# A compare tree over 36 chunks, and paired word steps, as single VectorE instructions

## The chip, the cores and the metric

The kernel runs on one core of one Trainium2 chip. The metric is the device time of one execution in microseconds. The core has five engines with queues of their own: TensorE (PE, matmuls and their weight loads), VectorE (DVE), ScalarE (ACT), GpSimd (POOL) and SyncE (SP), and DMA queues started by some of them. Each engine runs its queue in order; a semaphore makes an instruction wait for another engine's.

## What is computed

Four graph layers run one after the other on 16 graphs of 1024 nodes with 64 channels. Each begins with a layer norm and a ReLU and ends with a residual. The change lies in the first layer's aggregation, which takes for each node and channel three quantiles of the neighbours' values:

```python
vals = jnp.where(nd[..., None], x[:, None, :, :], jnp.inf)   # nd: thinned adjacency
s = jnp.sort(vals, axis=2)
nv = nd.sum(2)
for tau, w in zip((0.25, 0.5, 0.75), (0.25, 0.5, 0.25)):
    pos = tau * (nv - 1)
    lo, hi = floor(pos), ceil(pos)
    agg = agg + w * (s[lo] + (pos - lo) * (s[hi] - s[lo]))
out = x + agg                        # then a two-layer MLP, masked
```

The other three are a gated message layer, a message layer with tanh, and an attention layer. All read the adjacency, of which some 6% is ones.

## The kernel before

The graphs are taken in eight pairs. For a pair, sort_begin and sort_pair sort each channel's 1024 node values on VectorE (one channel of one graph per partition): a bitonic sort of 55 steps, three instructions a step (L771 to L775), and then the same steps backwards on rank codes (L803 to L813). neighbours thins the adjacency and builds the 0/1 matrix ndT on all engines; it also writes a transposed copy of the adjacency (a_d, L886 and L887). weights turns rank codes into fp8 words wt (L974).

select then works on one graph at a time, eight tiles of 128 nodes, two tiles (TG) to a group, so four groups a graph. For each tile, words does this:

- 48 matmuls of ndT with wt (L1096): the bits of a word say which of 11 ranks are present, and the sum counts neighbours below. ScalarE evicts them into y (L1104), 128 values in each of 36 chunks (CHUNKS): 16 for each of two quantiles (full, NQ = 16), and 4 more (rest) that are joined with the first 16 at the end. Further matmuls make nat (L1124) and pz (L1132).
- 36 transposes of y (L1149), from which ScalarE makes two signs (L1151) for every eight chunks.

lasts runs on VectorE: it writes y plus 2048 beside y (L1162) and takes a tree of maxima over each chunk (L1167), down to one word in z per node, channel and one of four statistics. places turns z into four masks with some 26 instructions on 512 words (L1019, L1021, L1024): counts of the word's bits, three steps of a search for the place of the wanted rank. values multiplies the signs with tables (L1196; 40 matmuls for one statistic, 32 for the next) into candidates in PSUM, of which there are two buffers (pool sc), and VectorE picks from 12 candidates to one by copies under the masks (L1204) and adds it to agg (L1071, L1073). PSUM tiles named comb, of which there are four, hold the word sums, the transposes and the rest.

After the last words of a graph, compact gathers up to 64 exceptional nodes (L1235 to L1298, with 56 matmuls at L1287), and after both graphs extras treats them with their own maxima (L1007) and one call of places; its input comb_x is loaded on ScalarE's DMA queue (L1307), which also carries the stores of a_d. Then the four layers run for both graphs (L1459 and others read the adjacency as adjT), while neighbours, sort_pair and sort_begin of the next pairs run beside them.

The order on each engine is not written out by hand. The program states the work in order, with a priority, and a scheduler places every instruction on its engine's queue when its own model finds the operands ready; so the sort of the next pair stands in VectorE's queue between the instructions of select. The lines that set the order of the work around the change are these:

```python
now = words(0)
z = lasts(now[0])
for g in range(NT // TG - 1):
    values(g, now[1], places(sw, z, nf))
    now = words(g + 1)
    if g + 2 < NT // TG:
        z = lasts(now[0])
compact(b, i, wt, row10, out_of, kept, sw, sp)
values(g + 1, now[1], places(sw, lasts(now[0]), nf))
```

Of the kernel before, what the change touches and what calls it, by code (L numbers as in the profile page):

```python
# [13 lines left out]
U16 = mybir.dt.uint16  # L14
I16 = mybir.dt.int16
# [3 lines left out]
ALU = mybir.AluOpType  # L19
# [4 lines left out]
P = 128  # L24
# [18 lines left out]
def gnn_stack(ctx, tc, x, adj, nodemask, w, out):  # L43
# [952 lines left out]
    SHR, SHL, AND, XOR = ALU.logical_shift_right, ALU.logical_shift_left, ALU.bitwise_and, ALU.bitwise_xor  # L996
# [15 lines left out]
    def places(sw, z, nf, kept=2):  # L1012

        def word(name, bufs=1):
            return sw.tile([P, nf], U16, name=name, bufs=bufs)

        def bits(dst, src, v0, o0, v1=None, o1=None):
            if v1 is None:
                nc.vector.tensor_single_scalar(dst, src, v0, op=o0)  # L1019
            else:  # L1020
                nc.vector.tensor_scalar(dst, src, v0, v1, op0=o0, op1=o1)  # L1021

        def both(dst, p, q, op):
            nc.vector.tensor_tensor(dst, p, q, op=op)  # L1024

        zf = z.rearrange("p t s c -> p (t s c)")
        m, r, a, s0, s1, u1, u2 = (word(f"w_{n}") for n in ("m", "r", "a", "s0", "s1", "u1", "u2"))
        f1, f2, f, e0 = (word(f"w_{n}", kept) for n in ("f1", "f2", "f", "e0"))
        bits(m, zf, 1, SHL, 0xFFE, AND)
        bits(r, zf, 11, SHR, 31, XOR)  # L1030
        bits(s0, m, 1, SHR, 0x555, AND)
        both(a, m, s0, ALU.subtract)
        bits(s0, a, 2, SHR, 0x333, AND)
        bits(s1, a, 0x333, AND)
        both(s1, s0, s1, ALU.add)
        bits(s0, s1, 8, SHR)
        bits(s1, s1, 4, SHR, 15, AND)
        both(s1, s1, s0, ALU.add)
        both(u1.bitcast(I16), r, s0, ALU.subtract)
        both(u2.bitcast(I16), r, s1, ALU.subtract)  # L1040
        both(r, r, u1, ALU.min)
        both(r, r, u2, ALU.min)
        bits(f1, u1, 13, SHR, 4, AND)
        bits(f2, u2, 13, SHR, 4, AND)
        both(s0, f1, f2, ALU.add)
        both(m, m, s0, SHR)
        both(a, a, s0, SHR)
        bits(s1, a, 2, SHR, 3, AND)
        both(u1.bitcast(I16), r, s1, ALU.subtract)
        both(r, r, u1, ALU.min)  # L1050
        bits(f, u1, 14, SHR, 2, AND)
        both(m, m, f, SHR)
        bits(s0, m, 1, SHR, 1, AND)
        both(e0, s0, r, ALU.is_gt)
        return [v.rearrange("p (t s c) -> p t s c", t=z.shape[1], s=z.shape[2]) for v in (f2, f1, f, e0)]
# [25 lines left out]
    def select(b, i, wt, positive, ndT, row10, qb, qz, agg, kept, sw, sg, sy, sc, sp):  # L1081
        coef = row10[:, :, 3:9].rearrange("p t (k s) -> p t k s", s=2)
        if True:
# [74 lines left out]
            def lasts(ys):  # L1158

                z = sw.tile([P, TG, 4, C], U16, name="z", bufs=2)  # L1160
                for tl, y in enumerate(ys):
                    nc.vector.tensor_scalar_add(y[:, 1], y[:, 0], 2048.0)  # L1162

                    yu = y.bitcast(U16)
                    full, rest = yu[:, :, : 2 * NQ], yu[:, :, 2 * NQ :]
                    for v, n in ((full, 64), (full, 32), (full, 16), (full, 8), (rest, 64), (rest, 32), (rest, 16)):
                        nc.vector.tensor_tensor(v[:, :, :, :n], v[:, :, :, :n], v[:, :, :, n : 2 * n], op=ALU.max)  # L1167
                    zs = z[:, tl].rearrange("p (s k) c -> p s k c", k=2)
                    nc.vector.tensor_tensor(
                        zs[:, :, 1, :].rearrange("p s (q d) -> p s q d", d=4), full[:, :, NQ:, :4], full[:, :, NQ:, 4:8],  # L1170
                        op=ALU.max,
                    )
                    nc.vector.tensor_tensor(full[:, :, :NQ, :4], full[:, :, :NQ, :4], full[:, :, :NQ, 4:8], op=ALU.max)
                    for s in range(2):
                        nc.vector.tensor_tensor(
                            zs[:, s, 0, :].rearrange("p (m q d) -> p m q d", m=4, d=4),
                            full[:, s, :NQ, :4].rearrange("p (m q) d -> p m q d", m=4),
                            rest[:, s, :, :16].rearrange("p m (q d) -> p m q d", d=4), op=ALU.max,
                        )
                return z  # L1180
# [31 lines left out]
            nf = TG * 4 * C  # L1212
# [11 lines that stand above are left out]
# [77 lines left out]
    def extras(pr, kept, aggs, xs, xp):  # L1301
# [21 lines left out]
        for k in range(3):  # L1323
# [21 lines left out]
            nc.vector.tensor_tensor(zs, ev, od, op=ALU.max)  # L1345
            nc.vector.tensor_tensor(os_, od, ev, op=ALU.is_gt)
        marks = places(xs, z, 6 * C, 1)
        aggx = xs.tile([P, C], F32, name="agg_x")
        ag = aggx.rearrange("p (q d) -> p q d", d=4)
# [269 lines left out]
    for pr in range(pairs):  # L1619
        with tc.tile_pool(reuse_waits="tile", name="keep", bufs=1) as keep:  # L1620
            aggs = [keep.tile([P, NT, C], F32, name=f"agg{i}") for i in range(2)]
            kept = {
                "flag": [keep.tile([P, NT], U16, name=f"flag{i}") for i in range(2)],
                "vx": keep.tile([P, 9], F32, name="vx"),
            }
# [76 lines left out]
```

## Time and profile before

| | us |
|---|---|
| median of 3 runs (5891.88 to 5895.87) | 5891.98 |
| the profiled execution | 5867.21 |
| its span, first to last instruction | 5865.4 |
| VectorE busy (86%) | 5066.1 |
| TensorE busy (75%), its weight loads beside it | 4372.7 |
| ScalarE busy (65%) | 3801.4 |
| the tree, L1167, 896 instructions | 668.7 |
| the picks, L1204, 1536 instructions | 533.7 |
| granted TensorE clock, mean share of full speed | 0.84 |

Busy time is from one profiled execution. An instruction's duration runs from its start to its last write; the next one on the engine can start before that, so sums of durations come out above the time they fill. Lines such as L1167 are lines of the kernel before.

### The profile page before, as it was taken

The page shows a single profiled execution, that of the slowest core. Times are in us where ns is not written, and L with a number is a line of the kernel's source. Part 1 is how long each engine was busy: PE and PEld are TensorE (multiplying, and loading weights), DVE is VectorE, ACT ScalarE, POOL GpSimd, SP SyncE. Part 2 cuts the span into 40 slices and gives each one's busy share as a digit, 9 for nine tenths or more (in the row PEclk, how much of TensorE's full clock was granted, in tenths as well). Part 3 has the DMA queues.
Part 4 walks back from the last instruction along what each step waited for, and adds up shares of the span by engine and source line. Part 5 has one row for each costly group of instructions (what it writes and reads, how often), then busy time and mean ns, then how long its engine had stood idle before and what let it go on. Part 6 is the DMA issues. An engine that isn't in the chain of part 4 may idle for free.

```text
span 5865.4 us, 114417 instructions
## 1 busy us (share of the span) xinstructions
PE 4372.7 (75%) x45010; PEld 2736.6 (47%) x45010; DVE 5066.1 (86%) x13175; ACT 3801.4 (65%) x5752; POOL 180.9 (3%) x292
## 2 busy tenths in 40 slices
PE   1488677885868857788577876788677895878856
PEld 1355443554435544455434554355443554435532
DVE  9899888988899897998889988899888998877744
ACT  1587657676576855777567666677657775577724
POOL 3000000000000000000000000000000000000000
PEclk5699778997889968899689986899878997789967
DMA  4401273013631056210561125501264013620023
GB/s 127 125 27 41 89 221 116 27 31 124 207 98 36 20 156 217 63 40 29 172 203 45 37 77 168 172 35 34 89 206 132 27 32 120 208 81 19 11 88 127
DMA packets 524420, 568.23 MB, mean 97 GB/s; under 512 B 263808, under 2 KB 413568, under 8 KB 523872
## 3 DMA queue, kind: packets, MB, share of 16 engines
q1 hardware_dynamic: 381472, 476.43, 26.0%
q10 hardware_dynamic: 140064, 81.84, 4.6%
q8 instruction: 355, 5.82, 0.4%
q0 software_dynamic: 2336, 2.57, 0.2%
q14 instruction: 193, 1.58, 0.1%
HBM read 376.95 MB, written 183.76 MB: 96 GB/s over the span
## 4 chain that ended last, share of the span: by engine, by line
PE 27%; DVE 23%; ACT 14%; DMA 10%; issue 3%; SPq 0%; POOL 0%; ACTq 0%; DVEq 0%; POOLq 0%
PE comb L1096 7%; DVE y L1167 5%; PE cand L1196 4%; DMA adjT<-a_d 4%; PE bank L1459 4%; ACT sign L1151 3%; PE comb L1287 3%; DMA a_d<-at 2%; ACT y L1104 2%; DVE cand L1204 2%; DVE att L1570 2%; DVE adjT L1563 1%; DVE y L1162 1%; DVE cum L878 1%; DVE wt L974 1%
## 5 line engine op out<-in xcount | busy, mean ns | idle before, releaser
L1096 PE MATMUL comb<-wt,ndT 128*128 128x512 fp8e5 x6144 | 1422.3, 383 | 119.5 <-ACT sign L1151 98.1
L1104 ACT ACTIVATE y<-comb,qb 128x512 int16<-128x512 f32 x1152 | 742.5, 711 | 479.4 <-PE comb L1096 479.0
L1096 PEld LDWEIGHTS <-ndT 128*128 128x128 fp8e5 x6144 | 587.6, 98 | 837.4 <-issue 196.9
L1196 PE MATMUL cand<-vtab,sign 128*128 128x48 f16 (+1 forms) x18432 | 678.8, 192 | 60.9 <-DVE agg L1071 32.4
L1196 PEld LDWEIGHTS <-sign 128*128 128x128 fp8e5 x18432 | 651.5, 97 | 118.6 <-issue 57.2
L1151 ACT ACTIVATE sign<-comb,lower 128x1024 fp8e5<-128x1024 int16 (+1 forms) x640 | 693.2, 1083 | 0.0
L1151 ACT ACTIVATE sign<-comb,half 128x1024 fp8e5<-128x1024 int16 (+1 forms) x640 | 688.0, 1075 | 0.0
L1167 DVE TENSOR_TENSOR y<-y 128x512 uint16<-128x512 uint16 (+5 forms) x896 | 668.7, 788 | 16.6 <-PE comb L1149 16.2
L1204 DVE COPY_PREDICATED cand<-w_f,cand 128x256 f32<-128x256 uint16 (+1 forms) x1536 | 533.7, 376 | 95.8 <-PE cand L1196 92.6
L886 ACT COPY at<-pk 128x512 f32<-128x512 f32 x256 | 147.4, 586 | 394.5 <-PE pk L884 219.0
L1149 PE MATMUL comb<-ident_b,y 128*128 128x128 bf16 x4608 | 318.1, 222 | 93.5 <-ACT sign L1151 59.6
L1459 PE MATMUL bank<-adjT,nd 128*64 128x512 f32 x1024 | 314.1, 668 | 77.6 <-DMA adjT<-a_d 75.7
L1149 PEld LDWEIGHTS <-y 128*128 128x128 bf16 x4608 | 294.6, 99 | 118.9 <-issue 117.9
L928 PE MATMUL pk<-minus_b,rem 128*128 128x128 bf16 x1024 | 225.3, 246 | 158.2 <-ACT rem L909 158.2
L1459 PE MATMUL bank<-att,hs 128*64 128x512 f32 x512 | 199.9, 863 | 155.0 <-ACT hs L1575 154.9
L928 PE MATMUL pk<-ident_b,ni 128*128 128x128 bf16 x1024 | 220.5, 243 | 122.0 <-ACT ndT L934 65.0
L878 DVE TENSOR_TENSOR_SCAN cum<-ni 128x1024 f16<-128x1024 fp8e5 x128 | 291.8, 2283 | 11.0 <-POOL ni L874 10.9
L884 PE MATMUL pk<-ident,a 128*128 128x128 f32 x1024 | 189.5, 336 | 136.8 <-DMA a<-in_adj_dram 102.5
L974 DVE TENSOR_SCALAR wt<-node 128x2048 uint8<-128x2048 f16 x224 | 268.8, 1216 | 13.9 <-PE comb L1287 13.7
L774 DVE TENSOR_TENSOR s<-s 128x512 f32<-128x512 f32 (+1 forms) x440 | 275.6, 626 | 0.0
L1162 DVE TENSOR_SCALAR y<-y 128x4608 int16<-128x4608 int16 x128 | 173.4, 1355 | 118.0 <-ACT y L1104 117.7
L775 DVE TENSOR_TENSOR s<-s 128x512 f32<-128x512 f32 (+1 forms) x440 | 274.4, 624 | 0.0
(373 smaller groups left out, 8301.5 us busy)
## 6 DMA issues: line engine op xcount, KB each, us to landing
adjT<-a_d SPq DMA_DIRECT2D x384, 512.0 KB
a<-in_adj_dram SPq DMA_DIRECT2D x128, 512.0 KB
a_d<-at ACTq DMA_DIRECT2D x256, 256.0 KB
m_d<-swapped SPq DMA_DIRECT2D x104, 512.0 KB
swapped<-m_d SPq DMA_DIRECT2D x104, 512.0 KB
n_d<-nat SPq DMA_DIRECT2D x128, 128.0 KB
x_d<-xr SPq DMA_DIRECT2D x48, 256.0 KB
comb_x<-x_d ACTq DMA_DIRECT2D x24, 512.0 KB
```

Of the source, the lines that this page charges most:

```text
L774: nc.vector.tensor_tensor(to_lo, lo, hi, op=ALU.max)
L878: nc.vector.tensor_tensor_scan(cum[:, t - t0, :], ni[:, t, :], wide[:, t, pad - 1 : pad - 1 + N], 0.0, op0=ALU.add, op1=ALU.add)
L928: nc.tensor.matmul(pk[:, n % 4, :], lhs, rhs, start=(n % 4 == 0 and m == 0), stop=(m == len(terms) - 1 and last),)
L974: nc.vector.tensor_scalar(wt[g][:, :, k : k + 4, :].bitcast(U8), node, 4.0 * (25 + CODE * (8 * g + k)), 4.0 * 26, op0=ALU.add, op1=ALU.min,)
L1096: nc.tensor.matmul(pw, ndT[:, j, t * P : (t + 1) * P], wt[1 + g8][:, j].rearrange("p w c -> p (w c)"), start=(j == 0), stop=(j == NT - 1),)
L1104: nc.scalar.activation(y[:, 0, chunks, at : at + 8 * d_].rearrange("p q (w d) -> p q w d", d=d_), pw.rearrange("p (w q d) -> p q w d", w=8 ...
L1149: nc.tensor.transpose(pt[:, q - q0, :], y[:, 0, q, :].bitcast(BF16), ident_b)
L1151: nc.scalar.activation(signs[tl][s][:, q0:q1, :], pt.bitcast(I16), AF.Sign, bias=before[s], scale=-1.0, saturate=False,)
L1167: nc.vector.tensor_tensor(v[:, :, :, :n], v[:, :, :, :n], v[:, :, :, n : 2 * n], op=ALU.max)
L1196: nc.tensor.matmul(cand[:, e, at : at + 12 * d_].rearrange("p (d l) -> p d l", l=12), signs[tl][sec][:, chunk, :], tab[:, q, :, half_ * 12 ...
L1204: nc.vector.copy_predicated(v[:, :, :, dst : dst + k], mk.to_broadcast([P, 2, C // 2, k]), v[:, :, :, frm : frm + k])
L1459: nc.tensor.matmul(po[to : to + C, :], lhs, rhs[:, f * HALF : (f + 1) * HALF], start=(j == 0), stop=(j == NT - 1))
```

## The change

Three edits, all on VectorE:

- The tree's steps at 64, 32 and 16 run over all 36 chunks at once, where they ran over the 32 chunks of full and the 4 of rest in turn. The step at 8 stays as it is, since the chunks of rest end at 16 values.
- In places, m and a, s0 and s1, u1 and u2, f1 and f2 become the halves of four tiles of twice the width, and the two subtractions, the two sign extractions and the two shifts are one instruction each. The operand that both share, r or s0, is repeated with stride 0.
- Nothing else: the number of buffers stays (two for ff, f and e0; two PSUM tiles for the candidates), and so does the stated order of the work. The scheduler orders the queues anew for the changed list of instructions.

```diff
+        def two(name, bufs=1):
+            return sw.tile([P, 2, nf], U16, name=name, bufs=bufs)
+
+        def twice_(v):
+            return v.rearrange("p (o n) -> p o n", o=1).to_broadcast([P, 2, nf])
+
         zf = z.rearrange("p t s c -> p (t s c)")
-        m, r, a, s0, s1, u1, u2 = (word(f"w_{n}") for n in ("m", "r", "a", "s0", "s1", "u1", "u2"))
-        f1, f2, f, e0 = (word(f"w_{n}", kept) for n in ("f1", "f2", "f", "e0"))
+        r = word("w_r")
+        ma, ss, uu, ff = two("w_ma"), two("w_s"), two("w_u"), two("w_ff", kept)
+        m, a, s0, s1, u1, u2, f1, f2 = (v[:, k, :] for v in (ma, ss, uu, ff) for k in range(2))
+        f, e0 = (word(f"w_{n}", kept) for n in ("f", "e0"))
...
-        both(u1.bitcast(I16), r, s0, ALU.subtract)
-        both(u2.bitcast(I16), r, s1, ALU.subtract)
+        both(uu.bitcast(I16), twice_(r), ss, ALU.subtract)
         both(r, r, u1, ALU.min)
         both(r, r, u2, ALU.min)
-        bits(f1, u1, 13, SHR, 4, AND)
-        bits(f2, u2, 13, SHR, 4, AND)
+        bits(ff, uu, 13, SHR, 4, AND)
         both(s0, f1, f2, ALU.add)
-        both(m, m, s0, SHR)
-        both(a, a, s0, SHR)
+        both(ma, ma, twice_(s0), SHR)
...
                     full, rest = yu[:, :, : 2 * NQ], yu[:, :, 2 * NQ :]
-                    for v, n in ((full, 64), (full, 32), (full, 16), (full, 8), (rest, 64), (rest, 32), (rest, 16)):
+                    for v, n in ((yu, 64), (yu, 32), (yu, 16), (full, 8)):
                         nc.vector.tensor_tensor(v[:, :, :, :n], v[:, :, :, :n], v[:, :, :, n : 2 * n], op=ALU.max)
```

## The prediction

> **What bounds the kernel now.** I read the engine totals, then two stretches of the windows table, then the groups by shape, then the timeline of single engines, and last the order of the changed program's queues, which can be listed without running it. The profiled execution took 5867.2 us around a span of 5865.4; the median of the three timed runs is 5892.0, 0.4% above. I work in the profiled times and carry the difference over to the median.
>
> The totals (busy us, share of the span, instructions):
>
> ```profile
> PE 4372.7 (75%) x45010; PEld 2736.6 (47%) x45010; DVE 5066.1 (86%) x13175; ACT 3801.4 (65%) x5752; POOL 180.9 (3%) x292
> ```
>
> VectorE (DVE) is busiest, but an average hides that two kinds of group alternate in the selection stage. Two such groups, from the first L1162 of one to that of the next:
>
> ```profile
> core 0: us, PE busy (x) PEld busy (x) DVE busy (x) ACT busy (x) POOL busy (x), PEclk, DMA share, GB/s
> 378.60:419.70 41.10, 36.78 (x488) 24.21 (x488) 40.89 (x109) 33.17 (x55) 0.00 (x0) 1.00 0.06 21
> 5285.10:5324.00 38.90, 36.74 (x489) 24.27 (x489) 31.76 (x91) 33.40 (x55) 0.00 (x0) 1.00 0.03 8
> ```
>
> In the first ("dense") group the next pair's sort fills VectorE to 40.89 of 41.10 us: VectorE sets the period. In the second ("trailing") the sort has run out: VectorE idles 7 us, TensorE (PE) 2.2, and TensorE with its waits sets 38.9 us. The old queues hold 19 trailing groups (one in pair 0, two in each of pairs 1 to 6, six in pair 7); the other groups of pairs 0 to 6 are dense or hold a compaction.
>
> **What a merged instruction saves.** Mean ns per instruction stand after the bar; the run of seven is one whole old tree:
>
> ```profile
> L1167 DVE TENSOR_TENSOR y<-y 128x4096 uint16<-128x4096 uint16 x128 | 292.7, 2286 | 16.6 <-PE comb L1149 16.2
> ...
> L813 DVE TENSOR_TENSOR code<-code,xo 128x1024 uint16<-128x1024 uint16 x232 | 159.3, 686 | 4.1
> ...
> L1167 DVE TENSOR_TENSOR y<-y 128x512 uint16<-128x512 uint16 x256 | 105.1, 416 | 0.0
> ```
>
> ```profile
> 401.30 5.03 DVE L1167 TENSOR_TENSOR y<-y 128x4096 uint16<-128x4096 uint16 x7
> ```
>
> From 4096 and 512 elements: (2286 - 416) / 3584 = 0.522 ns an element, and 149 ns fixed. But the seven means of a tree add up to 5.52 us and the run lasts 5.03, so six successors each start 81 ns before the end of the one ahead. The issue slot's fixed part is 149 - 81 = 68 ns, and that, not 149, is what a merge saves. The change removes three instructions per tile in the tree (three pairs of seven become three of four; 128 tiles) and three per call of places (64 calls in selection, 8 in extras): 384 + 216 = 600, times 68 ns = 40.8 us of VectorE time. The elements stay. The operand repeated by stride 0 keeps its rate if it behaves as L813, which repeats one too and takes 686 ns for 1024 elements (0.522 x 1024 + 149 = 684).
>
> The Trainium skill (Perfetto Trace Analysis, Optimizing Scalar/DVE Operations) puts this overhead at about 60 ns, which would make 36 us, and advises grouping where the engine is saturated. The same section speaks against the change elsewhere: where VectorE is not saturated but holds up others, breaking instructions up may finish sooner; that is the trailing group.
>
> **What it adds: dependence.** The old tree alternated the 32 and the 4 chunks, so that no step followed the one it read. The new one is a bare chain. What such a pair costs is seen in the last extras, where nothing else was left to put between:
>
> ```profile
> 5619.85 0.25 DVE L1021 TENSOR_SCALAR w_r<-z_x 128x384 uint16<-128x384 uint16 x1
> 5620.02 0.25 DVE L1021 TENSOR_SCALAR w_s<-w_m 128x384 uint16<-128x384 uint16 x1
> 5620.30 0.36 DVE L1024 TENSOR_TENSOR w_a<-w_m,w_s 128x384 uint16<-128x384 uint16 x1
> ```
>
> w_s reads nothing of w_r and starts 0.17 us after it; w_a reads w_s and starts 0.28 us after it, though w_s took as long as w_r. A bare dependent pair loses 0.11 us. In the dense groups the new order puts a sort step or a pick between, so nothing is lost, but VectorE's order changes. In trailing groups nothing is left: a tree gains 3 x 0.068 and loses 3 x 0.11, so it ends some 0.1 us later. The Trainium skill (VectorE: DVE Perf Modes, The DRAIN you can't avoid) says a semaphore between vector operations costs nothing; by it the tree would end 0.2 us earlier, and the measured pair decides.
>
> **Dense groups.** VectorE loses 2 x 3 x 0.068 + 3 x 0.068 = 0.61 us a group, with as many sort instructions ahead of the second compaction as before (140 against 141 in the pair I counted). But the new queues also put V (L1196) later: after the 36 transposes (L1149) TensorE mostly runs 37 to 43 word matmuls (L1096) before the first 72 of V, where it ran 11 to 17, and VectorE takes the next L1162 in the middle of places. The next bound is TensorE: 36.78 busy, the waits on ScalarE that stay (0.28, 1.26 and 1.62 below) and some 0.6 at the second tile's transposes make 40.3; L1162 waits for the last eviction, and I take 40.6. That is 41.1 - 40.6 = 0.5 a group; bounds 0 and 0.61 x 2. Three groups ahead of the first compaction in seven pairs: -10.5 us. The group of that compaction and the one after it hold 0.61 each, and VectorE has idle time in the first; I take 1.0 a pair, -7 (bounds 0 and -14).
>
> **Trailing groups.** TensorE, first around the transposes of a dense group, then of a trailing one:
>
> ```profile
> 416.55 2.01 PE L1149 MATMUL comb<-ident_b,y 128*128 128x128 bf16 x32 [0.28 <-ACT y L1104]
> 419.82 0.38 PE L1149 MATMUL comb<-ident_b,y 128*128 128x128 bf16 x4 [1.26 <-ACT sign L1151]
> 421.83 3.90 PE L1096 MATMUL comb<-wt,ndT 128*128 128x512 fp8e5 x16 [1.62 <-ACT sign L1151]
> ```
>
> ```profile
> 5302.40 2.02 PE L1149 MATMUL comb<-ident_b,y 128*128 128x128 bf16 x32 [0.28 <-ACT y L1104]
> 5304.52 1.63 PE L1196 MATMUL cand<-vtab,sign 128*128 128x48 f16 x40
> 5305.98 0.39 PE L1149 MATMUL comb<-ident_b,y 128*128 128x128 bf16 x4
> 5306.99 0.96 PE L1196 MATMUL cand<-vtab,sign 128*128 128x48 f16 x32 [0.62 <-DVE agg L1073]
> 5307.80 2.92 PE L1096 MATMUL comb<-wt,ndT 128*128 128x512 fp8e5 x12
> ```
>
> The old trailing order hides the two sign waits behind V (40, then 32). The new order reads 36 transposes, V 40, 5 word matmuls, V 32, 12 word matmuls, in all its 24 groups of that kind (pairs 2 to 6 now have three). The last four transposes then wait for the first pair of signs, as in the dense group: about 5305.7. V's 40 end at 5307.2, the 5 words wait for the second pair (5307.7) and end at 5308.8. V's 32 need a candidate buffer. L1162 now stands ahead of the last steps of places and waits for the eviction until 5302.4; with its slot of 1.27, eight steps left of places and picks (1.7), the tree's first step (2.5) and one add (0.2) the second buffer comes free near 5308.1. So V starts at 5308.8 and ends at 5309.6, the 12 words at 5312.3. By the old order the same work (17 words) would be done at 5307.8 + 17 x 0.222 = 5311.6. The price is 0.7 us; bounds 0 and 2.3 (1.26 + 1.62 - 0.62). Nineteen groups: +13.3. Five groups change from dense (about 40.1) to this kind (39.6): -2.5.
>
> **Extras.** ScalarE's queue in pair 1:
>
> ```profile
> 1387.58 0.58 ACT L886 COPY at<-pk 128x512 f32<-128x512 f32 x1 [0.89 <-PE pk L884]
> 1389.11 0.58 ACT L886 COPY at<-pk 128x512 f32<-128x512 f32 x1 [0.95 <-DMA a_d<-at]
> 1389.14 0.96 ACTq L887 DMA_DIRECT2D a_d<-at  x2
> 1390.13 2.69 ACTq L1307 DMA_DIRECT2D comb_x<-x_d  x4
> ```
>
> The load of comb_x is issued behind eight copies and eight a_d stores; in the new order behind seven copies and six stores, the other two following it. It can go at about 1388.2, 2 us sooner, and ScalarE idles 10.9 us for it. Behind it wait the extras, then the layers, but the neighbours' work on ScalarE and the loads of a and adjT share that path; I take half, -1 in seven pairs, -7 (bounds 0 and -14). Extras' own places: 8 x 0.2 less some stalls, -1.
>
> **The sum.** -10.5 - 7 + 13.3 - 2.5 - 7 - 1 = -14.7 us: 5852.5 profiled, 5877 on the median.
>
> **Rivals.** (a) VectorE is the path everywhere that counts: all 40.8 us come off, 5851. For it, 86% busy; against it, the 7 us idle in trailing groups and over 45 in each pair's layers. (b) Slower: V behind the transposes exposes both sign waits in full, 24 x 2.3 = +55, with -28 of gains left, +27, 5919. It decides above (28 + 12) / 24 = 1.7 us a group; against it, the walk above, by which the second wait is mostly covered. (c) The change does not do what it says: an instruction with a repeated operand falls to one element a cycle. The subtraction and the shift, 2 x 1024 x 0.52 ns x 64 = +68 us, 5960. L813 speaks against it. (d) All is absorbed, 5892: gains end in L1162's wait for ScalarE.
>
> **How the numbers follow.** About 0.2% (12 us) is what a measurement of this kernel can tell from no change. Forecast 0.48, own range 5860 to 5892: 0.33 of it faster by over 0.2%, 0.15 within. (a) 0.13, faster. (d) 0.12, same. (b) 0.23 and (c) 0.04, slower. So faster 0.46, same 0.27, slower 0.27. The range for 8 in 10 reaches to (a) with a little more from comb_x below, 5846, and most of (b) above, 5912.
>
> **What would show it.** Right: 68 ns per merge (tree instructions of 4608, 2304 and 1152 elements near 2553, 1351 and 750 ns); dense groups near 40.6 us with VectorE waiting for L1104 at the shift; trailing ones near 39.6 with 1.3 us of sign wait ahead of the last four transposes; comb_x issued 2 us sooner. Wrong: dense groups at 41 or more, trailing ones at 38.9 or above 40.5, places instructions of 1024 elements near 1.2 us, or layers stretches that differ by more than 3 us a pair.

## The result and the profile after

The changed kernel takes 5984.7 us (median of 6 runs, 5980.5 to 5992.4) against 5889.3 us for the kernel before in the same session: 1.0164 times as long, 95% interval 1.0151 to 1.0177. The forecast was 5877, the range 5846 to 5912. The change is slower by 95 us, and the profiled span grew by 114.1 us, from 5865.4 to 5979.5. Lines behind L1058 stand five higher in the changed kernel (L1167 became L1172, L1096 L1101, L1149 L1154, L1196 L1201).

The totals after the change (busy us, share, instructions):

```profile
PE 4464.2 (75%) x45010; PEld 2767.7 (46%) x45010; DVE 5052.1 (84%) x12575; ACT 3810.5 (64%) x5754; POOL 185.6 (3%) x292
```

VectorE has its 600 instructions less, but its busy time fell by 14 us only, not 41. TensorE is busy 91.5 us longer with the same 45010 matmuls. A dense and a trailing group, from the first shift (L1167) of one to that of the next, as shown of before:

```profile
core 0: us, PE busy (x) PEld busy (x) DVE busy (x) ACT busy (x) POOL busy (x), PEclk, DMA share, GB/s
3258.40:3299.80 41.40, 37.51 (x485) 24.17 (x483) 40.56 (x104) 33.28 (x55) 0.00 (x0) 0.96 0.07 26
5395.52:5435.34 39.82, 36.82 (x488) 24.22 (x488) 31.96 (x82) 33.34 (x55) 0.00 (x0) 1.00 0.03 9
```

The dense group varies with the sort instructions in it, and its mean with where it is cut. Cut like this, the two groups of pairs 0 to 6 that lie whole between a pair's first group and its compaction took 41.4 us in the mean and take 42.1; cut from second shift to second shift, the groups ahead of a compaction took 41.5 and take 40.7. The trailing one went from 38.90 to 39.82, close to the 39.6 forecast. And the merged shapes:

```profile
L1172 DVE TENSOR_TENSOR y<-y 128x4608 uint16<-128x4608 uint16 x128 | 326.7, 2552 | 65.6 <-PE comb L1154 65.5
L1172 DVE TENSOR_TENSOR y<-y 128x2304 uint16<-128x2304 uint16 x128 | 173.0, 1351 | 0.9
L1172 DVE TENSOR_TENSOR y<-y 128x1152 uint16<-128x1152 uint16 x128 | 96.1, 751 | 0.9
L1024 DVE TENSOR_TENSOR w_u<-w_r,w_s 128x1024 int16<-128x1024 uint16 x64 | 43.9, 685 | 1.0
L1024 DVE TENSOR_TENSOR w_ma<-w_ma,w_s 128x1024 uint16<-128x1024 uint16 x64 | 43.6, 682 | 0.0
L1021 DVE TENSOR_SCALAR w_ff<-w_u 128x1024 uint16<-128x1024 uint16 x64 | 26.7, 417 | 0.0
```

Every duration that was forecast came within 2 ns, the two instructions with a repeated operand (w_u and w_ma, 684 by L813) included. What is new stands behind the second bar of the first line: the tree's first step waits 65.5 us for the transposes, where it waited 16.2.

To see where the time went I cut the span at the shifts (L1162, one per tile and graph) into stages: the six tile intervals of each pair ahead of its compaction; the three from the compaction on; the other five; and the layers with the next pair's first tile. All of it in us, from one profiled execution of each kernel; stretches whose instructions and order are unchanged vary by up to some 12 us in sum between executions. The last stage but one begins at a pair's last shift, so it also holds the last tree of the pair, two of its nine calls of places, the second graph's compaction and the extras.

| | start | ahead of compaction | compaction | other five | layers, next first tile | tail | sum |
|---|---|---|---|---|---|---|---|
| before | 316.7 | 995.6 | 706.2 | 797.8 | 2730.3 | 318.9 | 5865.4 |
| forecast of the change | | -10.5 | -7 | +10.8 | -8 | | -14.7 |
| measured | -2.6 | -19.1 | +49.1 | +16.5 | +75.9 | -5.8 | +114.1 |

Two stages went as forecast and two went the other way, +49 and +76. Of the 76, 61 are the layers themselves and 15 the next pair's first tile, into which the new order puts 38 sort instructions instead of 34 in most pairs.

### The profile page after: what moved, and what is told of

Its sections match the earlier page's. It is cut to its first block, busy times and chain, and to the rows that moved or that the text cites. A ratio compares the mean times of both kernels' runs of the same rounds, so it can differ in the third digit from the quotient of the medians.

```text
span 5979.5 us, 113851 instructions
## 1 busy us (share of the span) xinstructions
PE 4464.2 (75%) x45010; PEld 2767.7 (46%) x45010; DVE 5052.1 (84%) x12575; ACT 3810.5 (64%) x5754; POOL 185.6 (3%) x292
## 4 chain that ended last, share of the span: by engine, by line
DVE 36%; PE 35%; ACT 13%; DMA 10%; issue 4%; POOL 0%; SPq 0%; ACTq 0%; DVEq 0%; POOLq 0%
PE comb L1101 10%; PE cand L1201 6%; DVE y L1172 5%; DMA adjT<-a_d 4%; PE bank L1464 4%; PE comb L1292 4%; ACT sign L1156 3%; DVE cand L1209 3%; DVE cum L878 2%; DVE s L774 2%; DVE s L775 2%; ACT y L1109 2%; DVE swapped L773 2%; DVE att L1575 2%; DMA a_d<-at 2%
## 5 line engine op out<-in xcount | busy, mean ns | idle before, releaser
L1101 PE MATMUL comb<-wt,ndT 128*128 128x512 fp8e5 x6144 | 1451.0, 390 | 99.8 <-ACT sign L1156 88.1
L1101 PEld LDWEIGHTS <-ndT 128*128 128x128 fp8e5 x6144 | 598.1, 100 | 831.0 <-issue 219.9
L1201 PE MATMUL cand<-vtab,sign 128*128 128x48 f16 (+1 forms) x18432 | 673.4, 192 | 86.1 <-DVE agg L1076 49.9
L1201 PEld LDWEIGHTS <-sign 128*128 128x128 fp8e5 x18432 | 641.8, 97 | 164.9 <-issue 75.2
L1172 DVE TENSOR_TENSOR y<-y 128x4608 uint16<-128x4608 uint16 (+3 forms) x512 | 649.0, 1268 | 68.3 <-PE comb L1154 65.5
L1209 DVE COPY_PREDICATED cand<-w_ff,cand 128x256 f32<-128x256 uint16 x1024 | 418.8, 421 | 83.1 <-PE cand L1201 79.9
L1154 PE MATMUL comb<-ident_b,y 128*128 128x128 bf16 x4608 | 314.2, 221 | 105.0 <-ACT sign L1156 77.8
L1154 PEld LDWEIGHTS <-y 128*128 128x128 bf16 x4608 | 287.0, 99 | 129.0 <-issue 128.0
L878 DVE TENSOR_TENSOR_SCAN cum<-ni 128x1024 f16<-128x1024 fp8e5 x128 | 292.0, 2285 | 15.6 <-POOL ni L874 13.3
L1167 DVE TENSOR_SCALAR y<-y 128x4608 int16<-128x4608 int16 x128 | 173.4, 1355 | 121.1 <-ACT y L1109 121.1
```

The source lines that it names most:

```text
L878: nc.vector.tensor_tensor_scan(cum[:, t - t0, :], ni[:, t, :], wide[:, t, pad - 1 : pad - 1 + N], 0.0, op0=ALU.add, op1=ALU.add)
L1101: nc.tensor.matmul(pw, ndT[:, j, t * P : (t + 1) * P], wt[1 + g8][:, j].rearrange("p w c -> p (w c)"), start=(j == 0), stop=(j == NT - 1),)
L1154: nc.tensor.transpose(pt[:, q - q0, :], y[:, 0, q, :].bitcast(BF16), ident_b)
L1201: nc.tensor.matmul(cand[:, e, at : at + 12 * d_].rearrange("p (d l) -> p d l", l=12), signs[tl][sec][:, chunk, :], tab[:, q, :, half_ * 12 ...
L1209: nc.vector.copy_predicated(v[:, :, :, dst : dst + k], mk.to_broadcast([P, 2, C // 2, k]), v[:, :, :, frm : frm + k])
```

## The experiments

### Which edit, and is it the edit or the order

Four kernels left the scheduler free. Tree only, then places only (both as in the change), then places merged in extras alone:

```diff
# e1_tree
-  for v, n in ((full, 64), (full, 32), (full, 16), (full, 8), (rest, 64), (rest, 32), (rest, 16)):
+  for v, n in ((yu, 64), (yu, 32), (yu, 16), (full, 8)):
# e3_extras_only: the merged places as places_x, called in extras alone
-  marks = places(xs, z, 6 * C, 1)
+  marks = places_x(xs, z, 6 * C, 1)
```

> Only the tree is merged; the steps of places stay as before. By stages the change cost, from the first shift of one tile to that of the next: -5 us ahead of the compactions, +49 in the three half-groups from the compaction on, +17 in the other groups, +61 in the layers. Theory O (the queue order): the tree alone puts V behind the 36 transposes, so trailing groups go to 39.8 us and the other groups cost +15; a tree step of 2.55 us stands in the way of the compaction's short steps, +28 or more (3.5 for each of 8); the layers' queues are ordered anew, so their sum moves by more than 20 us, either way. Theory W (the merged instructions cost what the change costs, where they stand): the layers hold no tree to speak of and stay within 7 us of 2450; compactions +30, the others +15; 5930.

> Only the steps of places are merged (selection and extras); the tree stays as before. Theory O: the trailing groups keep the old order of TensorE (40 of V ahead of the last four transposes) and stay at 38.9 us; the layers' queue is, by its landmarks, that of the whole change, and costs +50 to +70 us; compactions about 0 to +20. In all 5940 to 5980. Theory W: three merges a call cannot cost the layers anything (24 instructions fewer, 1.6 us): layers within 7 us of before, total 5870 to 5895.

> Only the eight calls of places in the extras are merged, 24 instructions fewer in 13000; selection has all its old instructions. Theory O: the layers' queues are ordered anew by this alone, and their sum moves by more than 20 us either way (up to +60), while the groups stay within 10 us. Theory W: -1.6 us, no difference that can be measured: 5889.

The fourth merges nothing. It states the seven tree steps of the kernel before in another sequence:

```diff
# e4_same_work
-  for v, n in ((full, 64), (full, 32), (full, 16), (full, 8), (rest, 64), (rest, 32), (rest, 16)):
+  for v, n in ((full, 64), (rest, 64), (full, 32), (rest, 32), (full, 16), (rest, 16), (full, 8)):
```

> The kernel before with the same seven tree instructions in another sequence (full 64, rest 64, full 32, rest 32, full 16, rest 16, full 8): no instruction is added, removed or changed in size. Theory O: the scheduler orders the layers' queues anew, and the sum of the layers moves by more than 20 us either way. Theory W: same time within 0.2%, layers within 7 us.

Measured, as ratio to the kernel before: e1 1.0074 (1.0053 to 1.0094), e2 1.0069 (1.0044 to 1.0094), e3 0.9978 (0.9964 to 0.9992), e4 0.9859 (0.9838 to 0.9881). So both edits lose, extras' alone gains 0.2%, and the same instructions in another sequence gain 1.4%, more than any of these three edits moves. Theory O's large shift of the layers came in e2 (+61.9 with the next first tile) and in e4 (-79.9), not in e1 (+11.5, with +19.8 in the compaction and +13.5 in the other five) nor in e3 (+6.2). In e2 almost the whole loss is in that stage, which holds two of a pair's nine merged calls. Order had to be held apart from merging.

For that, every engine's queue was pinned. An edge that is no wait ties each instruction to the one ahead of it, by a table written into the kernel:

```python
for i in mine[at : at + n]:          # one engine's instructions, in the order wanted
    if behind is not None:
        tc.add_manual_dep(i, behind.name, edge, reason="queue order")   # edge: NoSync
    behind = i
```

First the two crossed cases (e5: the changed kernel's instructions in before's order; e6: before's in the new order), then the merged steps one kind at a time in before's order:

```diff
# the tree's steps; before: (full, 64), (full, 32), (full, 16), (full, 8), (rest, 64), (rest, 32), (rest, 16)
# e8: places merged as in the change, the tree as before
# e9, places as before
+  for v, n in ((yu, 64), (full, 32), (full, 16), (full, 8), (rest, 32), (rest, 16)):
# e10 and e11, places merged
+  for v, n in ((full, 64), (rest, 64), (yu, 32), (yu, 16), (full, 8)):
```

> The changed kernel's instructions, each engine's queue held by issue-order edges to the sequence of the kernel before (a merged instruction stands where the later of its two stood; the rest of its tree follows it). Theory O (the loss is the queue order): the merges now show their own worth, 0.61 us in each group in which VectorE is the limit: 20 to 45 us faster than before, 5835 to 5860, with the layers within 10 us of before. Theory W (the merged instructions cost it): +60 to +114 stays, compactions +40 above all.

> The reverse: every instruction of the kernel before, in the sequence of the changed kernel (the two halves of a merged instruction one behind the other in its place). Theory O: slower than the changed kernel by the 20 to 40 us that the merges are worth, 6000 to 6030, with compactions, trailing groups and layers all dearer as in the changed kernel. Theory W: as before, within 10 us of 5880.

> The kernel before with places merged (216 instructions fewer), every queue held to the order of before. Free to be ordered anew, the same edit cost 61 us, all of it in the layers with their first group. Theory O: with the order held, that loss is gone, and what is left is the worth of the merges, 3 x 0.068 us a group where VectorE is the limit: 0 to 15 us faster, 5858 to 5873 against 5873. Theory W: the 61 us stay.

> The kernel before with only the first step of the tree merged (64 over all 36 chunks; 128 instructions fewer), every queue held to the order of before; the later steps stay apart. Theory T (the merged first step must wait for the transposes of the last four chunks, for which the old first step over 32 chunks left time): 2.3 us at each trailing tile of the four-chunk wait and some in dense groups, most of the 172 us that the whole change costs in this order: 100 to 180 slower. Rival S (the cost in this order is the bare chain of merged steps, spread over all of them): at most a third, 0 to 60 slower.

> The complement: places merged and the tree's steps at 32 and 16 merged, the first step apart (full, then rest); 472 instructions fewer, every queue held to the order of before. Theory T: no new wait, so the worth of the merges shows: 10 to 30 us faster than before, 5843 to 5863. Rival S: slower by half of the 172 or more.

And the whole change (e7) and e10's merges (e11) in e4's order:

> The changed kernel's instructions in the queue order that the kernel with the old tree in another sequence had (5797 us there). Theory O: 20 to 40 us below that, 5755 to 5780, the fastest so far. Theory W: 5797 + 95, near 5890.

> The same merges as in the kernel ahead of this, in the queue order of the kernel that has the old tree in another sequence (1.4% faster than before with no merge at all). Theory T: 10 to 30 us below that, 5760 to 5785, faster than both kernels by 1.6 to 2%. Rival S: 5850 or more.

| kernel | instructions | order | ratio (95%) | ahead of comp. | comp. | other five | layers, first tile |
|---|---|---|---|---|---|---|---|
| changed | merged | new | 1.0164 (1.0151 to 1.0177) | -19.1 | +49.1 | +16.5 | +75.9 |
| e6 | before's | new | 1.0181 (1.0146 to 1.0217) | -16.6 | +47.1 | +14.4 | +63.5 |
| e5 | merged | before's | 1.0309 (1.0267 to 1.0351) | +60.3 | +23.9 | +91.4 | +3.4 |
| e8 | places merged | before's | 0.9995 (0.9982 to 1.0007) | +10.5 | -0.1 | -0.8 | +10.0 |
| e9 | tree's first step merged | before's | 1.0245 (1.0228 to 1.0263) | +49.8 | +24.9 | +78.1 | +19.1 |
| e10 | places, later tree steps merged | before's | 1.0077 (1.0061 to 1.0094) | +25.0 | +5.6 | +17.4 | +11.9 |
| e4 | before's | e4's | 0.9859 (0.9838 to 0.9881) | +5.4 | +0.4 | +9.3 | -79.9 |
| e11 | e10's | e4's | 0.9880 (0.9861 to 0.9898) | +1.5 | +0.5 | +16.4 | -77.2 |
| e7 | merged | e4's | 1.0069 (1.0047 to 1.0091) | +22.7 | +34.5 | +51.4 | -56.1 |

Three things follow. The new order costs all of the loss without one merged instruction (e6: +1.8%, stage by stage the change's own row to 13 us). What the merges are worth in the new order cannot be told from nothing: 2.5 us ahead of the compaction, less than an unchanged stage varies. And in the old order the change would be worse still (e5: +3.1%), for the most part because of one edit, the tree's first step (e9: +2.45%).

Of the expectations, those of e8 (theory O) and e9 (theory T) came out. The gain that O or T put on the merges came in none of e5, e7, e10 and e11, nor does e6 lose the 20 to 40 us more than the changed kernel that O gave it; the rivals' figures did not come there either. No run pins the kernel before to its own order; the nearest to it, e8 and the later e14 (one exchange, 1.0011), show no cost of the pinning.

**Why the first step costs.** Its merged form reads all 36 chunks, so it waits for the last four transposes too, and in the old trailing order 40 matmuls of V stand between the 32 and the four. e9's group, then VectorE's timeline from the shift to the tree in a trailing tile of before and of after:

```profile
L1167 DVE TENSOR_TENSOR y<-y 128x4608 uint16<-128x4608 uint16 x128 | 326.9, 2554 | 105.0 <-PE comb L1149 105.0
```

```profile
5323.97 1.36 DVE L1162 TENSOR_SCALAR y<-y 128x4608 int16<-128x4608 int16 x1 [4.33 <-ACT y L1104]
5326.05 4.57 DVE L1167 TENSOR_TENSOR y<-y 128x4096 uint16<-128x4096 uint16 x5 [0.71 <-PE comb L1149]
```

```profile
5395.50 1.36 DVE L1167 TENSOR_SCALAR y<-y 128x4608 int16<-128x4608 int16 x1 [3.69 <-ACT y L1109]
5399.22 3.95 DVE L1172 TENSOR_TENSOR y<-y 128x4608 uint16<-128x4608 uint16 x2 [2.36 <-PE comb L1154]
```

From shift to tree it was 2.08 us and is 3.72; the wait in brackets grew from 0.71 to 2.36. The scheduler's answer to that is the new order: V behind all 36 transposes, in the trailing groups of e1 as in the changed kernel, and not in e2. It leaves 65.5 us of that wait instead of 105, and the new order itself costs e6's +1.8%. In the new order the wait is not what costs: e6 has the step apart and next to none of it, and is no faster than the changed kernel:

```profile
L1167 DVE TENSOR_TENSOR y<-y 128x4096 uint16<-128x4096 uint16 x128 | 292.5, 2285 | 15.6 <-PE comb L1149 15.6
```

The Trainium skill's advice weighed in the prediction (Perfetto Trace Analysis, Optimizing Scalar/DVE Operations), to break instructions up where VectorE is not saturated but holds up others, points the same way as e9's other five (+78.1). Ahead of the compaction, where VectorE is nearly full and the same section would group, the merged step lost 49.8 us as well.

**Why the other merges gain nothing.** The slot saved is real, but where the chain is bare it pays it back. A bare tree from its first step to L1169 took 5.07 us before (the seven steps alternate), 5.23 in the changed kernel and 5.30 in e10, which starts like this:

```profile
5379.64 5.27 DVE L1172 TENSOR_TENSOR y<-y 128x4096 uint16<-128x4096 uint16 x5 [0.71 <-PE comb L1154]
```

If all 128 trees lost these 0.23 us it would be 29 us, of the 46 by which e10's median is above e8's; the rest is not accounted for. In places, where nothing stands between its steps, the first pick comes 0.11 us later in e8 (5.37 us behind the first step instead of 5.26), although two instructions fewer stand ahead of it.

### What the new order costs in the compaction

VectorE in one compaction (pair 3), before, then after:

```profile
2559.64 1.36 DVE L1162 TENSOR_SCALAR y<-y 128x4608 int16<-128x4608 int16 x1
2560.92 0.17 DVE L1235 TENSOR_REDUCE f<-out_of 128x8 f32<-128x24 f32 x1
...
2567.00 1.22 DVE L1257 TENSOR_TENSOR sel<-count,at 128x1024 f32<-128x1024 f32 x1
```

```profile
2599.91 1.36 DVE L1167 TENSOR_SCALAR y<-y 128x4608 int16<-128x4608 int16 x1 [0.49 <-ACT y L1109]
...
2603.83 0.17 DVE L1240 TENSOR_REDUCE f<-out_of 128x8 f32<-128x24 f32 x1
...
2608.53 2.55 DVE L1172 TENSOR_TENSOR y<-y 128x4608 uint16<-128x4608 uint16 x1
...
2613.28 1.22 DVE L1262 TENSOR_TENSOR sel<-count,at 128x1024 f32<-128x1024 f32 x1
```

From the shift to the selection matrix it took 7.4 us and takes 13.4. The compaction is a ping-pong of short steps between VectorE and TensorE. With V late, the picks of the last tile stand ahead of its first VectorE step (3.9 us instead of 1.3 behind the shift), and V stands ahead of its matmuls on TensorE:

```profile
2606.95 0.17 PE L1252 MATMUL comb<-fb,below 128*128 128x8 bf16 x1 [0.23 <-ACT sign L1156]
2608.47 0.40 PE L1201 MATMUL cand<-vtab,sign 128*128 128x48 f16 x9 [1.34 <-DVE agg L1078]
2608.70 0.17 PE L1253 MATMUL comb<-fb,ones_b 128*128 128x8 bf16 x1
```

L1253 reads nothing of V and comes 1.75 us after L1252: nine matmuls of V stand between them and wait 1.34 us for a candidate buffer. In e6, without a merged step, this stage costs +47.1: it is the order. How the 6 us divide between the picks and V was not tried.

### What the new order costs in the layers

Two halves first, then the second half cut again, each as before's instructions in before's order but for one stretch of each pair:

> Every instruction of the kernel before, in the order of before, but for one stretch of each pair: from the last tile's shift to the start of the layers proper (the rest of the compaction, extras, most of neighbours; some 160 us) the queues have the order of the changed kernel. The layers with their first group cost +63 to +76 in that order as a whole. Theory F (the extras' load that goes out earlier displaces neighbours, and the delay is met later): +40 or more here. Theory G (the interleaving of the two graphs' layers with each other and the sort's end): within 15 us of before, 5870 to 5890.

> The complement: the order of before up to the start of the layers proper, that of the changed kernel from there to the first tile of the next pair. Theory F: within 15 us of before. Theory G: +40 to +65, 5920 to 5945, with the second layer's end and the third layer's start 2 to 9 us later in each pair.

> The kernel before, every instruction as it stands there, and every queue in its order, except that in the seven stretches of the layers proper the changed kernel's order stands from the start of the message layer to the end of the gated one (167 to some 255 us after a pair's last shift). Theory E (early exchanges delay the gated layer, and what follows is only late): most of the +109 us of the run with the whole stretch is here, +60 to +100 us over the kernel before. Theory L (the second message layer and the attention carry the loss, where the sort steps, the neighbours' transposes and the next pair's words stand among the layers' short steps): +10 to +40 us, as the first landmark behind it, L1523, is 3.6 us a pair later there. E and L would both fall if this and its complement each cost under 30.

> The complement: before's instructions and before's order, except that the changed kernel's order stands from the end of the gated layer (some 255 us after a pair's last shift) to the next pair's first tile. Theory E: under 30 us over the kernel before. Theory L: +65 to +100 us, with the second message layer's L1544 and the next pair's 48th word matmul late by 5 and 11 us a pair. If neither, the two halves hurt only together.

| new order only | ratio (95%) | layers and next first tile |
|---|---|---|
| e12: last shift to the layers proper | 1.0074 (1.0055 to 1.0092) | +32.8 |
| e13: layers proper to the next first tile | 1.0186 (1.0167 to 1.0205) | +108.8 |
| e16: e13's part up to the gated layer's end | 1.0050 (1.0033 to 1.0066) | +34.6 |
| e17: e13's part behind it | 1.0119 (1.0102 to 1.0136) | +94.4 |

Neither F nor G came out as stated: the medians rose by 39 us in e12, where G had at most 15, and by 105 in e13, where F had at most 15 and G at most 65. The parts add to more than the 76 of the whole: the junctions seem to cost something of their own (in e17 the next pair's words wait 18.8 us in all for VectorE's L1566, which has no match in the changed kernel). Theory L of e16 and e17 holds: the larger part stands behind the gated layer. The changed kernel's landmarks say the same. Counted from a pair's last shift, the mean of seven pairs is later by 1.5 us at the second graph's selection matrix, 2.2 at the end of the extras, 4.1 at the end of the gated layer, 11.0 at the attention's first weighted rows and 8.7 at the next pair's first shift. So some 15 of the 76 us arise ahead of the layers proper.

Two exchanges could be read off the timelines. The first, in e16's stretch, is on ScalarE. Before, then after:

```profile
2955.66 0.59 ACT L1501 ACTIVATE two<-bank 64x512 f32<-64x512 f32 x1 [2.47 <-PE bank L1459]
2956.88 0.59 ACT L886 COPY at<-pk 128x512 f32<-128x512 f32 x1 [0.62 <-DMA a_d<-at]
2957.49 0.37 ACTq L887 DMA_DIRECT2D a_d<-at  x1
```

```profile
3012.01 0.59 ACT L886 COPY at<-pk 128x512 f32<-128x512 f32 x1 [5.03 <-DMA a_d<-at]
3012.62 0.37 ACTq L887 DMA_DIRECT2D a_d<-at  x1
3013.03 0.59 ACT L1506 ACTIVATE two<-bank 64x512 f32<-64x512 f32 x1 [0.44 <-ACT at L886]
```

The copy waits for a buffer that a store holds, 5.03 us, and the layer's activation now stands behind it. Two runs move that one instruction, once into the kernel before and once out of the changed one:

```diff
# ScalarE's queue, six pairs; e14: before -> this. e15: the reverse, in the changed kernel
-  L1501 two, L886 at, L887 a_d
+  L886 at, L887 a_d, L1501 two
```

> The kernel before, every instruction and every queue's order as it stands there, except one exchange on ScalarE in six of the seven pairs: the layers' first activation of two (L1501) is put behind the next copy of pk into at (L886) and its store (L887), as the changed kernel's queue has it. No step is merged. Theory S (this exchange is the layers' loss): the copy waits some 5 us for an earlier store, L1501 and the gate matmuls L1509 behind it wait too, L1509's idle time before ScalarE's two goes from 9.8 us to about 25, the layers with the next first tile lose 30 to 75 us, the whole is 20 to 60 us slower than the kernel before. Rival (many exchanges share the loss): L1509's idle time rises, but the whole is within 15 us of the kernel before.

> The changed kernel, every instruction and every queue's order as it stands there, except that the layers' first activation of two (L1506) is put back ahead of the copy of pk into at and its store, as the kernel before has it, wherever the changed kernel has it behind them. Theory S: L1514's idle time before ScalarE's two falls from 25.8 us to about 10, the layers with the next first tile fall by 25 to 60 us, the whole is 5925 to 5960 us against 5985 for the changed kernel. Rival (many exchanges share the loss): the idle time falls, but the whole stays within 12 us of the changed kernel.

The gate matmuls, from the groups of before, e14, the changed kernel and e15 (busy, mean ns | idle time and what ended it):

```profile
L1509 PE MATMUL bank<-gates,two 128*128 128x256 f32 x256 | 80.0, 435 | 11.5 <-ACT two L1501 9.8 <-DVE two L1502 1.6
```

```profile
L1509 PE MATMUL bank<-gates,two 128*128 128x256 f32 x256 | 83.9, 453 | 20.9 <-ACT two L1501 19.8 <-DVE two L1502 1.0
```

```profile
L1514 PE MATMUL bank<-gates,two 128*128 128x256 f32 x256 | 92.6, 486 | 27.9 <-ACT two L1506 25.8 <-DVE two L1507 1.8
```

```profile
L1514 PE MATMUL bank<-gates,two 128*128 128x256 f32 x256 | 82.1, 435 | 21.5 <-ACT two L1506 14.7 <-DVE two L1507 6.6
```

The wait goes where the exchange goes, 9.8 to 19.8 and 25.8 to 14.7. The layers follow by less: +15.6 us in e14's profile, and in e15's +47.4 is left of +75.9. The times say less still: e14 1.0011 (0.9993 to 1.0028), 6 us; e15 1.0144 (1.0127 to 1.0162) against 1.0164, 12 us by the ratios and 21 by the medians. Theory S's 20 to 60 us of the whole were not reached in e14, nor its 5925 to 5960 in e15 (5963.9). The exchange is a part, 16 and 28 of 76 us by the two profiles, 6 to 21 by the times; e15's profiled execution is the fastest of its four; the rival, many exchanges, is nearer.

The second exchange, in the attention, stands behind the gated layer. VectorE of e15, where it is still in:

```profile
3078.93 0.17 DVE L945 TENSOR_SCALAR last<-pk 128x8 f32<-128x8 f32 x1 [5.72 <-PE pk L938]
...
3080.25 1.28 DVE L1575 SCALAR_TENSOR_TENSOR att<-adjT,top,att 128x1024 f32<-128x1024 f32 x1
```

A step of the next pair's neighbours waits 5.72 us for TensorE at the head of the queue, with the attention behind it. e18 undoes this one too:

```diff
# the changed kernel with e15's edit, six pairs
# VectorE:  -  L945 ... L956, L1575, L1575, L1578, L957, L1578
#           +  L1575, L1575, L1578, L1578, L945 ... L956, L957
# ScalarE:  -  L1537, L853, L1539, L1580, L1580
#           +  L1580, L1580, L1537, L853, L1539
```

> The changed kernel, every instruction as it stands there, and every queue in its order but for two exchanges undone in six of the seven pairs: the first (as in e15) on ScalarE, L1506 ahead of a copy and a store of a_d; and the second, in the attention, where the changed kernel's VectorE queue has the next pair's L945 to L956, which wait for TensorE's L938, ahead of the first two blocks' L1575 and L1578, and ScalarE's queue has L1537, L853 and L1539 ahead of the two L1580 that follow them. Here L1575, L1578 and L1580 stand ahead, as in the kernel before. Theory A (this block at the head of VectorE's queue holds the attention up): VectorE reaches L1575 some 4.5 us sooner a pair, the first two weighted rows hs (L1580) come 4 to 7 us sooner, the layers fall by another 20 to 40 us below e15's, the whole is 5922 to 5947 us against e15's 5964 (ratio to the kernel before 1.007 to 1.011). Rival D (diffuse: the wait only moves to TensorE's order or to the transfers of adjT): within 10 us of e15, 5954 to 5974.

```profile
3072.59 1.28 DVE L1575 SCALAR_TENSOR_TENSOR att<-adjT,top,att 128x1024 f32<-128x1024 f32 x1 [2.30 <-ACT att L1574]
3075.20 0.15 DVE L945 TENSOR_SCALAR last<-pk 128x8 f32<-128x8 f32 x1
```

```profile
3081.55 2.43 ACT L1566 ACTIVATE adjT<-adjT,fdst 128x1024 f32<-128x1024 f32 x2 [3.33 <-DMA adjT<-a_d]
```

The wait at L945 is gone, and the first weighted rows come 3.9 us sooner behind the attention's start (9.5 us after L1561, 13.4 in e15; mean of six pairs). The next blocks then wait 3.33 us for their transfer of adjT, and by the second pair of blocks nothing is left (23.3 us against 23.4). e18 takes 1.0113 (1.0088 to 1.0139), its median 5958 against e15's 5964, while its profiled span is 13 us longer. By the ratios it is 18 us less, but the two intervals overlap: no gain that is clear of noise. The median lies outside theory A's 5922 to 5947 and within D's 5954 to 5974; the ratio, 1.0113 where A had up to 1.011, does not exclude A. The trace speaks for D: a long wait was taken away, and what followed was late again.

So the cause of the +76 is shown to be the order, and one exchange carries at most some 28 of it; which others carry the remaining 48 or more stays open.

### Where e4's gain is

The first tile of a pair, before and in e4:

```profile
1686.90:1728.49 41.59, 28.06 (x223) 15.52 (x224) 39.85 (x73) 29.68 (x50) 0.00 (x0) 0.75 0.21 66
```

```profile
1690.90:1709.29 18.39, 15.50 (x138) 8.96 (x138) 18.36 (x31) 17.66 (x33) 0.00 (x0) 1.00 0.07 15
```

Before, 34 sort instructions of the next pair stand in this tile's VectorE queue; in e4 11 do, and the tile takes 18 us instead of 42. The rest went into the trailing groups, where VectorE idled 7 us each; that stage costs 9 us more in all. Over the seven pairs the first tiles give 121 us and the layers take back 41. That is -1.4% without one instruction changed, 5796.8 us, faster than both kernels; with the later merges on top (e11) it is no better.

## Why the prediction was wrong, step by step

**The saving per merge: right in size, wrong in worth.** The shapes ran at 2552, 1351 and 751 ns against 2553, 1351 and 750, so rival (c) is out. But "In the dense groups the new order puts a sort step or a pick between, so nothing is lost" assumed the gain. Whatever stands between them there, e6 against the changed kernel shows 2.5 us in these groups, less than such a stage varies by itself. In before's order the merges gain nothing either: e8 equal within 0.2%, e10 slower. The Trainium skill (VectorE: DVE Perf Modes, The DRAIN you can't avoid) measured no extra cost of a semaphore between vector operations; the prediction's estimate from it, a tree that ends 0.2 us earlier, does not fit here: 5.07 us became 5.23.

**Dense groups: the stage's sum about right, by luck.** -19.1 measured for -10.5, within the bounds. It came with the order (e6 alone -16.6), not from VectorE's shorter work, and all of it is in the first interval of the stage, from a pair's second shift to its third (20.5 us, now 17.8), while the tile ahead of that takes 1.7 us more. Cut as the prediction cut them, the groups went from 41.4 to 42.1 us: 41 or more was its own sign of being wrong. (Its 36.78 us and the waits come to 40.5, not 40.3; the 40.6 that it took does not depend on that.)

**Trailing groups: right.** 39.82 us against 39.6; the last four transposes wait for their signs as the walk had it:

```profile
5412.86 2.02 PE L1154 MATMUL comb<-ident_b,y 128*128 128x128 bf16 x32 [0.28 <-ACT y L1109]
5416.14 0.38 PE L1154 MATMUL comb<-ident_b,y 128*128 128x128 bf16 x4 [1.26 <-ACT sign L1156]
5416.83 1.63 PE L1201 MATMUL cand<-vtab,sign 128*128 128x48 f16 x40 [0.30 <-DVE agg L1076]
5418.29 1.24 PE L1101 MATMUL comb<-wt,ndT 128*128 128x512 fp8e5 x5
```

The price is 0.92 us a group instead of 0.7, and +16.5 for the stage instead of +10.8. Rival (b)'s mechanism, both sign waits in full, did not come; its side of the result did.

**A wait that was missing: the first step's.** I costed the merged step by its elements and never asked which semaphores it inherits. It waits for whichever of the 32 and the four transposes ends last: 65.5 us in the new order and 105 in the old, where it was 16.2. In the old order the step with that wait makes most of e5's loss (e9); in the new one it is no term of the loss, since e6 has 15.6 us of it and loses as much. What came with it in the result is the order of the trailing groups, which e1 has too.

**The compaction: the sign was wrong, -7 against +49.** The text took the saved slots there, "VectorE has idle time in the first", and did not walk the compaction's steps through the new queues. I had seen that V moves behind the transposes, and followed what it passes in dense and trailing groups only.

**Extras and layers: -8 against +76.** I looked at one queue (comb_x on ScalarE, "2 us sooner") and took the layers as unchanged since no edit touches them. The comb_x step brought nothing: in the mean of pairs 1 to 6 its first load stands at 52.5 us after a pair's last shift instead of 52.9, and extras end 1.8 us later, not sooner. The queues of the layers, which carry the next pair's neighbours and sort between their steps, were reordered throughout, and that is the largest term of the result.

## What to carry to other kernels

When a scheduler places the instructions, an edit's first effect is a new order of everything, also of stages that it does not touch: walk the new queues through every stage, or hold the order and time the edit alone, before any saved slot is counted. A merged instruction inherits all the waits of its parts, and it takes away the independent neighbour that filled the gap of a dependent pair; on VectorE here, 68 ns saved against 0.11 us lost. A long wait on a trace is a cause only when taking it away moves the end: of the two exchanges tried, undoing the one with the 5.7 us wait moved the end by nothing clear of noise.

## What the runs showed of the hardware beyond that

The same 45010 matmuls kept TensorE busy 4372.7 us before, 4464.2 in the changed kernel and 4453.8 in e6, which has before's instructions. In the layers (165 to 315 us after a pair's last shift, mean of pairs 1 to 6) the granted clock was 0.839 before, 0.831 in e5, 0.805 in the changed kernel and 0.802 in e6, and the gate matmuls took 435, 486 and 490 ns (before, changed, e6). The profiles of all kernels held to before's order in this stretch, e14 with its one exchange among them, give 0.827 to 0.839; those of the changed kernel and of e6, e13 and e15 to e18, with the new order in all or part of it, 0.795 to 0.819. So order alone moves the granted clock too. Whether the lower clock made part of the layers' loss or followed from the other timing was not tried. In e15 the gate matmuls are back at 435 ns with their wait shortened, which does not part the two.
